# Four half units instead of three in each expert job beside the first layer

## The chip, the core and the metric

The kernel runs as one program on one core of a Trainium2 chip. The metric is the device time of one execution in microseconds (us), from the host's launch to the result in memory; lower is better. The core has five engines that run their own instruction streams in order and wait for one another through semaphores: PE (matmul; PEld is its weight load), ACT (ScalarE: activation functions), DVE (VectorE), POOL (GpSimd) and SP (SyncE, which issues nearly all DMAs here, in order).

## What is computed

The reference is a network of two layers on x of shape (4, 32, 96, 256), that is 4 batches of 3072 tokens with 256 channels. Cut to what matters:

```python
# layer 0: group norm, a selective-scan block along the 96 steps, then one along the 32 variables
x = x + conv(gn(x))
# layer 1: additive attention in each batch (3072 queries x 3072 keys, 32 hidden units)
t = tokens(x)
h = tanh(q[:, :, None, :] + k[:, None, :, :] + bh)
t = t + softmax(h @ Wa + ba) @ ln(t)
# then a mixture of 4 experts on ln(t), gated by graph attention over 1048576 edges
for e in range(4):
    hh = gelu(xn @ W1[e] + b1[e])            # 256 -> 512
    out = out + gate[e] * (hh @ W2[e] + b2[e])   # 512 -> 256
t = t + out
```

An expert's output without its gate depends on attention's result alone. Gates need the whole graph, and so all four batches.

## The kernel before

All arithmetic of the parts told of here is in float32. One program order is written out by hand for PE, ACT, DVE and POOL: generators hand out small steps, and the order in which they are called is the order on each engine.

**Stages.** Layer 0 works in 64 blocks of 384 tokens: for each batch eight blocks "t" (along the 96 steps) and eight blocks "d" (along the 32 variables); the first "t" block of the next batch stands before a batch's "d" blocks. Batch 0 runs alone. From then on attention of batch b runs beside layer 0 of batch b+1. `Attention.units` goes through 768 units a batch ("an entry"), each of them one tanh of 128x3072 on ACT (line 905) into one of three `th` buffers; the scores that read it (matmuls of line 878) are issued two units later. Each block of layer 0 has 48 slots, and a slot of layer 0 is issued beside one attention unit, half a slot at a time. When layer 0 is done, attention's fourth entry runs on with the sorting of edges on DVE (`Edges.sort`) and with `Experts.early`. Then the tail.

**Three places where experts are computed.** The 12288 tokens are 24 blocks of 512 tokens, and a unit is one block with one expert, 24 x 4 = 96 units in all.

- `Beside` (lines 1563 to 1660) is called at the end of every slot of layer 0. It holds at most one job at a time: (batch, expert, j). A job covers three half units, that is three times 256 tokens. At slot 31 of a block `choose` takes the next job, if the next entry's keys are not yet being made, the present entry's column is at least 40, and the job's batch is older than the present entry; the job then runs through slots 0 to 31 of the next block. It has no memory of its own for weights: W1 and W2 of the expert lie in columns 0 to 2047 of the 3072 columns of `krep`, the keys' place of the next entry, the transposed tokens `xt` and the bias `b2` in that entry's `qsel`. The hidden values `h` (3 half units x 4 x 256 columns) lie in `uab`, which the front of the next layer-0 block uses again from slot 32 on. `PRODUCTS` names the slots in which the matmuls of half a hidden layer (8 instructions in the trace) are issued (line 1637), one slot later DVE adds b1 and moves them to `h` (line 1624); after the second of a half unit `fetch` (line 1613) loads the next 256 tokens into the one `xt`. At slot `GELU` one activation goes over the whole of `h` (line 1643). `OUTPUTS` names the slots for the second layer (line 1648), one slot later DVE adds b2 (line 1629) and SP stores 128 KB to `kept`.
- `Experts.early` takes units of the first three batches that no job has done, in pairs with one expert, in entry 3. Weights lie in the unused `krep`; an expert is loaded when it changes, and this counts 4.0 us in the step's own pacing. Each pair ends with a `yield None`; the step runs until attention is done and the pair then begun is finished.
- The tail runs what is left: `tail` (lines 1821 to 1921) has an order by steps t, three steps a unit: PE's hidden layer and ACT's GELU in the unit's own three, PE's output layer one step later. The first units of a block whose gates are not there in time are stored to `kept` (line 1795 moves them); later ones are gated at once (lines 1798 and 1808). Between units stand the edges: per step so many gathers on POOL (line 1425, and 1127), one-hot products (lines 1465 to 1479) and, after each quarter of the edges, the gates of a batch (`gates_of`). When a batch's gates are there, each kept block of it is loaded (2 MB `all`, 512 KB `y`), added up on DVE with 16 operations (line 1808) and stored; two buffers each.

**What sets the number of jobs.** 12 half units a batch and expert give 4 jobs; two batches and four experts 32 jobs. Entry 1 has room for 13 jobs and entry 2 for 12, so 25 are run: 75 half units, 37 whole units. `early` then runs 22 units (11 pairs, three experts), and 37 stay for the tail, of which 17 are kept and 20 gated at once; 19 blocks are kept.

**Expert places.** `expert_places(t)` gives columns 0 to 1023 of a `krep` to W1 and 1024 to 2047 to W2; 1024 columns are free, which `early` uses in part for b2 and `Beside` not at all.

Of the kernel before, what the change touches and what calls it, by code (L numbers as in the profile page):

```python
# [21 lines left out]
AF = mybir.ActivationFunctionType  # L22
# [4 lines left out]
P = 128  # L27
B, NV, S, C = 4, 32, 96, 256
TOK = NV * S
M = B * TOK  # L30
NT = TOK // P
KC = C // P
# [18 lines left out]
HEADS, NEXP, FF = 4, 4, 512  # L51
# [10 lines left out]
HALVES = 3.0, 9.0  # L62
# [4 lines left out]
TB = 512  # L67
NQ, FC, NBLK_X = TB // P, FF // P, M // TB
# [5 lines left out]
class Layer0:  # L74
# [8 lines left out]
    def __init__(self, ctx, tc, ident, a, x1):  # L83
        self.nc, self.tc = tc.nc, tc
        self.ident, self.a, self.x1 = ident, a, x1
        pool = lambda name, bufs, **k: ctx.enter_context(tc.tile_pool(name=name, bufs=bufs, **k))
        self.const, self.wk, self.st = pool("l0c", 1), pool("l0w", 1), pool("l0s", 2)
        self.ps, self.ps_u = pool("l0p", 1, space=PSUM), pool("l0u", 1, space=PSUM)
        self.dram = pool("l0d", 1, space=bass.MemoryType.DRAM)
        self.ps_x = pool("l0x", 1, space=PSUM)  # L90
        self.turn, self.beside, self.dctx = 0, None, ctx.enter_context(ExitStack())
        self.dA = self.decay_places(True)
        self.lctx = ExitStack()
        alone = lambda name, **k: self.lctx.enter_context(
            tc.tile_pool(name=name, bufs=1, side="right", **k))
        self.ld, ps_l = alone("ldw"), alone("ldp", space=PSUM)
        self.dA.append(ps_l.tile([P, 1024], F32, tag="dA2", name="dA2"))
        self.lead_psum = lambda: ps_l.tile([P, 512], F32, tag="py", name="py")[:, :T]
        self.xt = [self.dram.tile([KC, P, NV, S], F32, tag="xt", name="xt", bufs=3)
                   for _ in range(B)]  # L100
        self.group_norm()
# [275 lines left out]
    def back(self, blk, then):  # L377
# [39 lines left out]
        def inputs(e, j):  # L417

            def f():
                if shared(j):  # L420
                    return
                dB = z["dB", j] = st.tile([P, SB, T], F32, tag="dB", name="dB", bufs=1)
                nc.vector.tensor_tensor(dB, blk["bB"].pop(j),  # L423
                                        z["dtu"].unsqueeze(1).to_broadcast([P, SB, T]), ALU.mult)
                fetch("bB", j)
            return f

        def inputs_beside(e, j):

            def f():  # L430
                dB = z["dB", j] = self.ld.tile([P, SB, T], F32, tag="dBl", name="dB", bufs=2)
                nc.gpsimd.tensor_tensor(dB, blk["bB"].pop(j),
                                        z["dtus", e].unsqueeze(1).to_broadcast([P, SB, T]), ALU.mult)
                fetch("bB", j)
            return f
# [16 lines left out]
        def outputs(j):  # L452
            def f():
                h = z["h", j]
                nc.gpsimd.tensor_tensor(h, h, blk["bC"].pop(j), ALU.mult)  # L455
                fetch("bC", j)
            return f
# [1093 lines left out]
def expert_places(t):  # L1551

    n = KC * FF
    return (t[:, :n].rearrange("p (k f) -> p k f", k=KC),
            t[:, n:n + FC * C].rearrange("p (k c) -> p k c", k=FC))


def load_expert(nc, a, e, w1, w2):
    nc.sync.dma_start(w1, a["W1"][e].rearrange("(k p) f -> p k f", p=P))
    nc.sync.dma_start(w2, a["W2"][e].rearrange("(k p) f -> p k f", p=P))  # L1560


class Beside:
# [2 lines left out]

    PRODUCTS = {0: (0, 0), 3: (0, 1), 5: (1, 0), 8: (1, 1), 10: (2, 0), 12: (2, 1)}
    GELU = 14  # L1570
    OUTPUTS = {15: (0, 0), 17: (0, 1), 20: (1, 0), 23: (1, 1), 26: (2, 0), 29: (2, 1)}

    def __init__(self, ctx, tc, a, l0, att, xn2T, dram):
        self.nc = nc = tc.nc
        self.a, self.l0, self.att, self.xn2T, self.dram = a, l0, att, xn2T, dram
        pool = ctx.enter_context(tc.tile_pool(name="l0e", bufs=1))
        self.o = lambda: pool.tile([P, C], F32, tag="eo", name="eo")
        self.b1 = pool.tile([P, NEXP, FC], F32, tag="eb1", name="eb1")
        nc.sync.dma_start(self.b1, a["b1"])
        self.half = TB // 2  # L1580
        n = TOK // self.half // 3
        self.jobs = [(b, e, j) for b in range(B - 2) for e in range(NEXP) for j in range(n)]
        self.kept, self.done, self.job, self.there = {}, [], None, None

    def units(self):

        halves = {(2 * (b * TOK // TB) + 3 * j + k, e) for b, e, j in self.done for k in range(3)}
        return [(i, e) for i in range(NBLK_X) for e in range(NEXP)
                if (2 * i, e) in halves and (2 * i + 1, e) in halves]

    def choose(self, last):


        att = self.att
        self.job = None
        if (not self.jobs or last or att.asked > att.entry + 1 or att.col < 40
                or self.jobs[0][0] >= min(att.normed, att.entry)):
            return
        b, e, j = self.job = self.jobs.pop(0)
        place = att.krep[(att.entry + 1) % 2]  # L1600
        self.w1, self.w2 = expert_places(place)
        rest = att.qsel[(att.entry + 1) % 2]
        self.xt, self.b2 = rest[:, :KC * self.half].rearrange("p (k m) -> p k m", k=KC), rest[:, KC * self.half:]
        if self.there != (att.entry, e):
            self.there = att.entry, e
            load_expert(self.nc, self.a, e, self.w1, self.w2)
            self.nc.sync.dma_start(self.b2, self.a["b2_rep"][:, e, :])
        self.first = 2 * (b * TOK // TB) + 3 * j
        self.fetch(0)

    def fetch(self, k):
        m = (self.first + k) * self.half
        self.nc.sync.dma_start(self.xt, self.xn2T[:, :, m:m + self.half].rearrange("k p m -> p k m"))

    def __call__(self, slot, last):
        nc = self.nc
        if self.job:
            b, e, j = self.job
            if slot == 0:
                self.h = self.l0.wide("eh").rearrange("p (k f m) -> p k f m", k=3, f=FC)  # L1620
            if slot - 1 in self.PRODUCTS:
                k, f2 = self.PRODUCTS[slot - 1]
                for f in (2 * f2, 2 * f2 + 1):
                    nc.vector.tensor_scalar(self.h[:, k, f, :], self.ps[:, f % 2, :],
                                            self.b1[:, e, f:f + 1], None, ALU.add)
            if slot - 1 in self.OUTPUTS:
                k, q = self.OUTPUTS[slot - 1]
                o = self.o()
                nc.vector.tensor_tensor(o, self.ps[:, 0, :], self.b2, ALU.add)
                i, n = divmod(self.first + k, 2)  # L1630
                nc.sync.dma_start(self.kept_block(i)[:, 2 * n + q, e, :], o)
            if slot in self.PRODUCTS:
                k, f2 = self.PRODUCTS[slot]
                self.ps = self.bank()
                for f in (2 * f2, 2 * f2 + 1):
                    for c in range(KC):
                        nc.tensor.matmul(self.ps[:, f % 2, :], self.w1[:, c, f * P:(f + 1) * P],
                                         self.xt[:, c, :], start=(c == 0), stop=(c == KC - 1))
                if f2 and k < 2:
                    self.fetch(k + 1)  # L1640
            if slot == self.GELU:
                h = self.h.rearrange("p k f m -> p (k f m)")
                nc.scalar.activation(h, h, AF.Gelu)
            if slot in self.OUTPUTS:
                k, q = self.OUTPUTS[slot]
                self.ps = self.bank()
                for f in range(FC):
                    nc.tensor.matmul(self.ps[:, 0, :], self.h[:, k, f, q * P:(q + 1) * P],  # L1648
                                     self.w2[:, f, :], start=(f == 0), stop=(f == FC - 1))
            if slot == 31:  # L1650
                self.done.append(self.job)
        if slot == 31:
            self.choose(last)
# [10 lines left out]
class Experts:  # L1664
# [54 lines left out]
    def hidden(self, i, w1, f):  # L1719

        ph = self.bank(self.ps_h, [P, TB], "ph")
        for k in range(KC):
            self.nc.tensor.matmul(ph, w1[:, k, f * P:(f + 1) * P], self.xts[i][:, k, :],
                                  start=(k == 0), stop=(k == KC - 1))
            yield ph
# [464 lines left out]
```

## Time and profile before

| what | us |
|---|---|
| median of 3 runs | 15007.42 (15002.35 to 15027.46) |
| the profiled execution's own time | 15006.76 |
| its span in the profile | 15004.8 |
| ACT busy in the span | 12227.7 (81%) |
| PE busy | 11632.7 (78%) |
| DVE busy | 10437.2 (70%) |
| POOL busy | 9042.6 (60%) |
| tanh of attention (L905), 3072 of them | 8667.0 |
| first and last GELU of a job (L1643) | 5620.8 and 10987.8 |
| first GELU of a tail unit (L1805) | 13936.6 |
| first and last edge gather (L1425) | 13942.1 and 14789.7 |
| last addition of a kept block (L1808) | 14983.4 |

The table of groups has, for an expert job, the following (line, engine, operation, tiles, shape, count; busy us, mean ns; idle time just before them and what ended it):

```profile
L1648 PE MATMUL ex<-krep,eh 128*128 128x256 f32 x1200 | 333.5, 426 | 55.0 <-ACT eh L1643 54.4 <-DVE eo L1629 0.5
L1637 PE MATMUL ex<-qsel,krep 128*128 128x256 f32 x1200 | 313.1, 406 | 30.5 <-DMA qsel<-xn2T 26.6 <-DVE pT L977 2.2 <-DVE h L448 1.6
L1624 DVE TENSOR_SCALAR eh<-ex,eb 128x256 f32<-128x256 f32 x300 | 130.6, 477 | 23.3 <-PE ex L1637 23.3
L1629 DVE TENSOR_TENSOR eo<-ex,qsel 128x256 f32<-128x256 f32 x150 | 62.3, 416 | 4.7 <-PE ex L1648 4.3 <-DMA kept<-eo 0.4
L1643 ACT ACTIVATE eh<-eh 128x3072 f32<-128x3072 f32 x25 | 69.2, 2768 | 0.3
```

The counts tell how much is done: 25 GELUs are 25 jobs, 1200 matmul instructions are 16 for each of 75 half units. Blocks of layer 0 can be told apart in the trace by their 64 decays (L410): blocks 25 to 32 go from 3525.7 to 4972.9 us, blocks 41 to 48 from 6532.1 to 8081.4.

```profile
3525.70:4972.90 1447.20, 1103.43 (x9479) 413.66 (x9475) 1107.04 (x1497) 1429.09 (x1082) 1097.37 (x784) 0.89 0.50 152
6532.10:8081.40 1549.30, 1286.58 (x10232) 546.59 (x10232) 1156.44 (x1641) 1480.39 (x1105) 1093.82 (x785) 0.92 0.50 151
```

These are two lines of the table of busy time by stretch: the stretch, its length, then the busy time and number of instructions of PE, PEld, DVE, ACT and POOL, the granted TensorE clock, the DMA engines' share and GB/s. The first eight blocks have no jobs, the second eight have one each.

### The profile page before, as it was taken

How to read it: one execution, taken by the hardware profiler on the slowest of the kernel's cores; microseconds unless marked ns; L12 is line 12 of the kernel's file. 1: busy time of each engine (PE TensorE's matmuls, PEld its weight loads, DVE VectorE, ACT ScalarE, POOL GpSimd, SP SyncE). 2: the span in 40 equal slices, each digit the busy share in tenths (PEclk: the TensorE clock that was granted, in tenths of full speed). 3: DMA queues.
4: the chain of work that ended last, by engine and by line, in shares of the span. 5: the costliest groups of instructions: out<-in, count | busy, mean ns of one | idle time of the engine just before them, and what ended most of it. 6: DMA issues, size and time to landing. Idle time of an engine off the chain costs nothing.

```text
span 15004.8 us, 223310 instructions
## 1 busy us (share of the span) xinstructions
PE 11632.7 (78%) x86496; PEld 5146.9 (34%) x86496; DVE 10437.2 (70%) x14862; ACT 12227.7 (81%) x9485; POOL 9042.6 (60%) x6971
## 2 busy tenths in 40 slices
PE   5676656777777778888887787888877888888888
PEld 2333322222222323333333333333333344433544
DVE  7888887777777877777777877577767633311367
ACT  3454538999999889999999899999988899999121
POOL 5777777777777777767676677477640144100683
PEclk8988978888888888899999889899988999999999
DMA  6777764445454544555454444355531000000224
GB/s 207 227 230 233 239 203 142 150 151 153 150 152 153 161 152 147 152 149 153 150 154 156 149 150 152 105 153 151 152 115 44 15 16 10 24 23 23 59 54 136
DMA packets 1197826, 1986.83 MB, mean 132 GB/s; under 512 B 411984, under 2 KB 645072, under 8 KB 1194320
## 3 DMA queue, kind: packets, MB, share of 16 engines
q1 hardware_dynamic: 1169104, 1967.10, 42.8%
q0 software_dynamic: 27648, 5.36, 0.7%
q8 instruction: 680, 11.14, 0.3%
q14 instruction: 394, 3.23, 0.1%
HBM read 1864.71 MB, written 107.35 MB: 131 GB/s over the span
## 4 chain that ended last, share of the span: by engine, by line
ACT 17%; PE 16%; DVE 7%; POOL 5%; issue 4%; DMA 1%; SPq 0%; DVEq 0%; ACTq 0%; POOLq 0%
ACT th L905 12%; PE pe L878 8%; POOL gs L1425 3%; PE pv L984 3%; ACT dA L410 2%; DVE h L448 1%; ACT pr L968 1%; POOL gd L1127 1%; PE ptw L975 1%; PE po L1731 1%; PE pz L517 1%; PE pc L1322 1%; DVE y L1808 0%; PE ex L1648 0%; DVE dB L423 0%
## 5 line engine op out<-in xcount | busy, mean ns | idle before, releaser
L905 ACT ACTIVATE th<-krep,qsel 128x3072 f32<-128x3072 f32 x3072 | 8667.0, 2847 | 377.0 <-PE pe L878 359.0
L878 PE MATMUL pe<-th,wa_blk 128*32 128x384 f32 x49152 | 5050.1, 539 | 1587.7 <-ACT pr L968 1361.7
L455 POOL TENSOR_TENSOR h<-h,bC 128x768 f32<-128x768 f32 x2048 | 3759.8, 1837 | 2586.0 <-DVE h L448 2187.4
L448 DVE TENSOR_TENSOR_SCAN h<-dA,dB 128x384 f32<-128x384 f32 x3008 | 2707.8, 942 | 988.7 <-ACT dA L410 717.2
L878 PEld LDWEIGHTS pe<-th,wa_blk 128*32 128x32 f32 x49152 | 1459.3, 116 | 4154.1 <-issue 1974.4
L423 DVE TENSOR_TENSOR dB<-bB,dtu 128x768 f32<-128x768 f32 x1912 | 1811.9, 948 | 172.0 <-ACT dtu L498 137.2
L462 POOL TENSOR_TENSOR h<-h 128x768 f32<-128x768 f32 x752 | 1419.6, 1888 | 53.6
L410 ACT ACTIVATE dA<-dt,t_A 128x380 f32<-128x380 f32 x2048 | 1124.7, 570 | 386.2 <-DVE h L448 296.5
L474 PE MATMUL py<-h,ident 128*128 128x384 f32 x2176 | 944.7, 567 | 490.8 <-POOL h L455 490.7
L410 ACT ACTIVATE dA<-dt,d_A 128x372 f32<-128x372 f32 x2048 | 1102.3, 562 | 146.4 <-DVE h L443 107.9
L984 PE MATMUL pv<-xn,pT 128*32 128x257 f32 x18432 | 1101.0, 387 | 129.5 <-DVE pT L977 128.7
L1043 POOL TENSOR_SCALAR sf<-sel,f 128x32 f32<-128x32 f32 x384 | 144.7, 398 | 1583.9 <-ACT f L1039 1481.5
L443 DVE TENSOR_TENSOR_SCAN h<-dA,dB 128x768 f32<-128x768 f32 x544 | 948.3, 1751 | 153.2 <-ACT dA L410 87.7
L977 DVE COPY pT<-ptw 128x512 f32<-128x512 f32 (+1 forms) x768 | 419.3, 546 | 738.3 <-PE ptw L975 737.8
L984 PEld LDWEIGHTS pv<-xn,pT 128*32 128x32 f32 x18432 | 580.2, 111 | 704.9 <-DVE pT L977 256.1
L464 POOL TENSOR_TENSOR y<-y,h 128x384 f32<-128x384 f32 x752 | 783.2, 1042 | 59.0
L463 POOL TENSOR_TENSOR h<-h 128x384 f32<-128x384 f32 x752 | 780.7, 1038 | 58.9
L474 PEld LDWEIGHTS py<-h,ident 128*128 128x128 f32 x2176 | 427.1, 212 | 970.1 <-POOL h L455 740.3
L961 DVE TENSOR_REDUCE nb<-pe 128x1 f32<-128x768 f32 x384 | 362.4, 944 | 405.7 <-PE pe L878 405.6
L1425 POOL DMA_INDIRECT gs<-tab_s,si x432 | 517.5, 1198 | 108.4 <-issue 108.4
L986 DVE COPY pvs<-pv 128x257 f32<-128x257 f32 x384 | 160.7, 419 | 603.4 <-PE pv L984 601.9
L1127 POOL DMA_INDIRECT gd<-tab_a,di x432 | 448.8, 1039 | 185.1 <-issue 182.0
(291 smaller groups left out, 15267.6 us busy)
## 6 DMA issues: line engine op xcount, KB each, us to landing
bB<-bc SPq DMA_DIRECT2D x2048, 384.0 KB
bC<-bc SPq DMA_DIRECT2D x2048, 384.0 KB
all<-kept SPq DMA_DIRECT2D x19, 2048.0 KB
x<-x SPq DMA_DIRECT2D x144, 256.0 KB
x<-x SPq DMA_DIRECT2D x192, 128.0 KB
xt<-xn2T SPq DMA_DIRECT2D x41, 512.0 KB
kept<-ko SPq DMA_DIRECT2D x39, 512.0 KB
qsel<-xn2T SPq DMA_DIRECT2D x75, 256.0 KB
```

The source lines that it names most:

```text
L410: nc.scalar.activation(inner(dA[:, s * T:(s + 1) * T] if alone else self.dA[s][:, :T]), inner(blk["dt"][:, e, :]), AF.Exp, scale=blk["w"][ ...
L423: nc.vector.tensor_tensor(dB, blk["bB"].pop(j), z["dtu"].unsqueeze(1).to_broadcast([P, SB, T]), ALU.mult)
L443: nc.vector.tensor_tensor_scan(flat(h), dA[:, :SB * T], flat(dB), 0.0, ALU.mult, ALU.add)
L448: nc.vector.tensor_tensor_scan(h[:, s, :], self.dA[s][:, :T], dB[:, s, :], 0.0, ALU.mult, ALU.add)
L455: nc.gpsimd.tensor_tensor(h, h, blk["bC"].pop(j), ALU.mult)
L462: nc.gpsimd.tensor_tensor(h0, h0, h1, ALU.add)
L464: nc.gpsimd.tensor_tensor(y[e], y[e], h0[:, 0, :], ALU.add)
L474: nc.tensor.matmul(z["py"], self.ident, h[:, s, :], start=(i == 0), stop=(i == DS - 1))
L878: nc.tensor.matmul(pe[q * QU:(q + 1) * QU, j, :KQ // 2], self.wa[:, k, :], th[:, c0:c0 + KQ // 2], start=(k == 0), stop=(k == NK - 1))
L905: nc.scalar.activation(th, s["krep"], AF.Tanh, bias=s["qsel"][:, col:col + 1])
L984: nc.tensor.matmul(pv[q * QU:(q + 1) * QU, :C + 1], pT[:, i, q * QU:(q + 1) * QU], s["xn"][:, q * NK + i, :], start=(i == 0), stop=(i == N ...
L1425: nc.gpsimd.indirect_dma_start(out=self.got[j][:, u, :], out_offset=None, in_=self.tab_s.rearrange("p n f -> (p n) f"), in_offset=bass.Ind ...
```

## The change

A job covers four half units. 12 half units a batch and expert give three jobs, so there are 24 jobs in all, twelve for each of the two batches. The hidden values of the fourth half unit do not lie in `uab` but in the last 1024 columns of the same `krep` that holds the expert's weights (`spare`, reached through `hidden(k, f)`). The GELU is two activations, one over the three half units in `uab` and one over `spare`, in slot 15 instead of 14. Products are issued in slots 0, 2, 4, 6, 8, 10, 11 and 13 (before: 0, 3, 5, 8, 10, 12), outputs in every second slot from 16 to 30 (before: 15, 17, 20, 23, 26, 29). The loads of `xt` follow the products of slots 2, 6 and 10. If all 24 jobs run, they cover 48 units; `early` chooses among 24 units, and with its 22 there are 26 for the tail.

```diff
-    PRODUCTS = {0: (0, 0), 3: (0, 1), 5: (1, 0), 8: (1, 1), 10: (2, 0), 12: (2, 1)}
-    GELU = 14
-    OUTPUTS = {15: (0, 0), 17: (0, 1), 20: (1, 0), 23: (1, 1), 26: (2, 0), 29: (2, 1)}
+    HALVES = 4
+    PRODUCTS = dict(zip((0, 2, 4, 6, 8, 10, 11, 13), ((k, f) for k in range(4) for f in range(2))))
+    GELU = 15
+    OUTPUTS = dict(zip(range(16, 32, 2), ((k, q) for k in range(4) for q in range(2))))
...
-        n = TOK // self.half // 3
+        n = TOK // self.half // self.HALVES
...
+        self.spare = place[:, KC * FF + FC * C:].rearrange("p (f m) -> p f m", f=FC)
...
-        self.first = 2 * (b * TOK // TB) + 3 * j
+        self.first = 2 * (b * TOK // TB) + self.HALVES * j
...
+    def hidden(self, k, f):
+        return self.h[:, k, f, :] if k < 3 else self.spare[:, f, :]
...
-                    nc.vector.tensor_scalar(self.h[:, k, f, :], self.ps[:, f % 2, :],
+                    nc.vector.tensor_scalar(self.hidden(k, f), self.ps[:, f % 2, :],
                                             self.b1[:, e, f:f + 1], None, ALU.add)
...
-                if f2 and k < 2:
+                if f2 and k + 1 < self.HALVES:
                     self.fetch(k + 1)
             if slot == self.GELU:
-                h = self.h.rearrange("p k f m -> p (k f m)")
-                nc.scalar.activation(h, h, AF.Gelu)
+                for h in (self.h.rearrange("p k f m -> p (k f m)"),
+                          self.spare.rearrange("p f m -> p (f m)")):
+                    nc.scalar.activation(h, h, AF.Gelu)
...
-                    nc.tensor.matmul(self.ps[:, 0, :], self.h[:, k, f, q * P:(q + 1) * P],
+                    nc.tensor.matmul(self.ps[:, 0, :], self.hidden(k, f)[:, q * P:(q + 1) * P],
                                      self.w2[:, f, :], start=(f == 0), stop=(f == FC - 1))
```

`units()` counts the finished half units with the same `HALVES`.

More of the change, by code (lines that the diff above doesn't have):

```diff
@@ L1585, in units @@
     def units(self):
-        halves = {(2 * (b * TOK // TB) + 3 * j + k, e) for b, e, j in self.done for k in range(3)}
+        halves = {(2 * (b * TOK // TB) + self.HALVES * j + k, e)
+                  for b, e, j in self.done for k in range(self.HALVES)}
         return [(i, e) for i in range(NBLK_X) for e in range(NEXP)
```

## The prediction

> **What bounds the kernel now.** I read the busy times by stage first, then the same table for the first 33 slots of four blocks, then what ScalarE waits for, then the chain of waits at the end. Columns of the tables: stretch, length, busy time (and instructions) of PE, PEld, DVE, ACT, POOL, then clock, DMA share, GB/s.
>
> ```profile
> 2200.00:5566.00 3366.00, 2448.32 (x20734) 958.90 (x20734) 2649.19 (x3655) 3159.88 (x2419) 2496.10 (x1781) 0.87 0.49 151
> 5566.00:11163.00 5597.00, 4507.69 (x36800) 1937.06 (x36804) 4153.44 (x5944) 5306.20 (x3913) 3828.89 (x2754) 0.90 0.49 148
> 11163.00:13936.60 2773.60, 2331.30 (x22861) 1048.86 (x22854) 1189.08 (x2096) 2520.78 (x1042) 442.79 (x757) 0.93 0.09 24
> 14733.50:15004.80 271.30, 223.90 (x676) 137.46 (x674) 196.52 (x407) 47.09 (x62) 48.67 (x43) 0.92 0.47 157
> ```
>
> Rows 1 and 2 are layer 0 beside attention, without and with expert jobs: ACT is busy 94 and 95%. Row 3 is attention alone with the early units. Row 4 is the tail from the first GELU of its 27th unit (14733.5). ACT rules until 13936, and there PE is next: 81% in row 2.
>
> ```profile
> 2620.20:2740.40 120.20, 91.32 (x826) 35.98 (x822) 92.61 (x120) 119.27 (x91) 93.25 (x68) 0.90 0.48 152
> 3707.90:3827.10 119.20, 98.89 (x830) 36.77 (x826) 88.65 (x120) 118.73 (x91) 92.38 (x66) 0.91 0.50 157
> 5566.10:5694.80 128.70, 109.20 (x890) 50.96 (x894) 96.83 (x138) 124.71 (x94) 92.27 (x67) 0.91 0.50 156
> 6726.50:6857.30 130.80, 117.45 (x902) 52.68 (x902) 94.77 (x137) 125.03 (x94) 92.26 (x67) 0.93 0.51 155
> ```
>
> Slots 0 to 32 of a "t" and a "d" block without a job, then with one. The job adds 8.5 and 11.6 us; PE's idle time falls from 28.9 to 19.5 ("t") and from 20.3 to 13.4 ("d"). ACT's idle time before tanh from 5566 to 11163 (what ended it, us, times):
>
> ```profile
>   PE pe L878: 163.9, 167
> ```
>
> The same row of 2240 to 5566, without jobs, says 25.4 us in 52 places. The first stretch has 1394 tanhs, the second 834; at the second's rate the first would wait 25.4 x 1394/834 = 42.5 us; the other 121.4 us, over 25 jobs (75 fetches of xt, 3 each), are **4.9 us a job** in which ScalarE waits for the matmuls that a job put ahead of attention's.
>
> **Stage B, one job fewer.** Blocks 41 to 48 ("d", jobs) last 1549.3/8 = 193.7 us, blocks 25 to 32 (none) 1447.2/8 = 180.9. Entry 1 now ends its 12 jobs at block 47, so block 48 has none: **-12** (bounds -11 and -13).
>
> **Stage B, the fourth half unit, 24 times.** ACT: GELU takes 2764 ns for 3072 columns (L1643) and 1909 for 2048 (L1767), so 855 per 1024 and some 0.2 for a second instruction: **1.05** a job (0.9 to 1.1). No further table load: both GELUs follow one another.
>
> ```profile
> 5619.46 1.28 ACT L1643 ACT_TABLE_LOAD   x1
> 5620.76 2.77 ACT L1643 ACTIVATE eh<-eh 128x3072 f32<-128x3072 f32 x1
> 5623.43 2.84 ACT L905 ACTIVATE th<-krep,qsel 128x3072 f32<-128x3072 f32 x1
> 5626.29 1.28 ACT L410 ACT_TABLE_LOAD   x1
> ```
>
> A job's fixed ACT cost is thus two loads, 2.6 us, with nothing idle around them; this is in the -12. The Trainium skill ("ScalarE: Activation LUTs", "What ACT_TABLE_LOAD costs") puts about 1.38 us of drain beside each 1.28 us load; the rows above show none, and by the rule the job saved would be worth 2.8 us more.
>
> PE: 16 matmuls more for products (313.1/75 = 4.2 us a half) and 16 for outputs (333.5/75 = 4.4): 8.6 us more in 33 slots that have 13 to 19 idle, part of it waiting for GELU (PE waits for L1643 54.4 us in 21 places) and not to be had. Proportionally ACT would wait 4.9/3 = 1.6 more a job; at worst all 8.6; at best nothing, if it all fits into the idle time. Waits grow faster than the load: I take **2.5**, nearer to the proportional row. The extra DVE work (4 x 0.48 + 2 x 0.42 = 2.8 us) lies in VectorE's 28% idle share; if that cover were gone it would cost up to 2.8 a job.
>
> The fetch of the fourth xt: issued after the products of slot 10 and used in slot 11, where earlier fetches had two slots. A fetch of today, two slots ahead:
>
> ```profile
> 5787.31 2.00 PE L1637 MATMUL ex<-qsel,krep 128*128 128x256 f32 x8
> 5789.85 2.85 ACT L905 ACTIVATE th<-krep,qsel 128x3072 f32<-128x3072 f32 x1
> 5790.55 0.42 SPq L1613 DMA_DIRECT2D qsel<-xn2T  x1
> 5793.60 2.85 ACT L905 ACTIVATE th<-krep,qsel 128x3072 f32<-128x3072 f32 x1
> 5795.02 1.75 PE L1637 MATMUL ex<-qsel,krep 128*128 128x256 f32 x7 [1.50 <-DMA qsel<-xn2T]
> ```
>
> The matmuls end at 5789.3, SyncE issues 1.2 us later (bC and xt stand ahead of it in its queue) and the data is there 4.5 us after that: 7.7 us from product to product, where one slot offers 3.75. PE stalls 2.8 to 4.0 us, about 3.4. Behind it in PE's queue stand the next scores (L878), for whose end tanh waits, with three th buffers of slack; in SP's queue the fetch holds up the bB and bC loads behind it until the products end, as each fetch does today (VectorE waits 4.6 us in all for bB in this stretch). Today's waits of 1 to 2 us hardly show in ACT; I take **1.0** of the 3.4 (bounds 0 and 3.4). The Trainium skill ("DMA: Bandwidth & Descriptors", "Anatomy of one DMA") fits about 2.0 us fixed plus bytes/436e3 per us, here 2.6 us, for copies issued by GpSimd; the row of this SyncE fetch says 4.5 under load and decides. By the rule the stall would be some 1.5 and I would take 12 us less.
>
> The two stores of eo more a job (8 for 6) go down SP's queue between bB and bC loads; DMA waits before L1629 are 0.4 us in all, so nothing, or up to 0.4 us x 24 if each costs as much as all do now. Expert loads stay 8 pairs (4 an entry). The spare place is part of the same krep tile as the weights: if the order is kept for whole tiles, products of slot 13 wait for the additions of slot 12 (0.9 us) and outputs of slot 16 for the second GELU (0.9); a slot lies between, so nothing, at most 1.8 a job. Sum B: -12 + 24 x (1.05 + 2.5 + 1.0) = **+97** (at best 24 x 0.9 - 13 = +9, at worst 24 x 13.1 - 11 = +303, the whole of PE's work on the path).
>
> **Stage C.** The early step has 24 units to choose from instead of 35 and runs 11 pairs as before, but in four experts instead of three: one load more, with 4.0 us in its own pacing; after the last tanh so much more of the pair is left to do: **+4** (0 to 10).
>
> **The tail.** Units 1 to 26 run in the same steps, so nothing falls away before 14733. Thereafter:
>
> ```profile
> 14769.25 4.09 DMA gs<-tab_s,si
> 14786.79 3.46 PE po L1731 x16
> 14806.24 3.43 PE ph L1723 x8
> 14864.43 11.53 DMA out<-y
> 14875.98 3.33 DMA y<-x
> ```
>
> The chain is the edge gather until 14769, then the last quarter's sums with unit matmuls pushed between (14786 to 14824: 3.46 + 3.43 + 1.72 + 3.46 = 12 us, their VectorE operations 3), then the last gates (until 14860; 6 us of unit operations among them). From there it is store, load of the next y, 16 additions (7.9 us) with two buffers: (11.5 + 3.3 + 1 + 7.9)/2 = 12 us a kept block. Nine and a half blocks remain at 14860, 114 us, today 124 between units' work. So of 11 units (15 us of PE each, 165) only 12 + 3 + 6 + 10 come off, and the last units' overhang of kept blocks (14984 to 14999), 15: 46. Against it 22 instead of 19 kept blocks: three more in the gather's stretch, 3 x 7.9 = 24 us of VectorE, of which I count 4 (0 to 15). **-42** (-25 to -60).
>
> Sum: 97 + 4 - 42 = **+59**; 15006.8 (the profiled execution, 0.6 below the median of the runs) + 59 = **15066**.
>
> **Rivals.** (1) Only proportional waits, 1.6 and 0.3 a job: B = -12 + 24 x 2.95 = 59, tail -50: 15006.8 + 59 + 4 - 50 = 15020. For it: today's DMA waits of PE are 26.6 us in 23 places. (2) PE becomes the bound of job blocks: in 15 "d" blocks 8.6 + 3.4 = 12 of 13.4 us idle would have to be usable. If ACT waits 8 of the 12 there and 5 in 9 "t" blocks, B = -12 + 24 x 1.05 + 165 = 178 and the time 15006.8 + 178 + 4 - 42 = 15147. Against it: PE's idle in "t" is 19.5. (3) **Faster**: PE's idle time swallows the half unit and the fetch (0 wait), at blocks 36 to 47 and 52 to 63: B +9, tail -60, C 0: 14956. It decides where a job adds under 2.1 us in all (12 + 42 - 4 over 24), that is under 1.0 of waiting. Against it: the 4.9 of today. (4) It doesn't do what it says: a job is not taken in time, or early ends a pair sooner (28 units): some +10 on the forecast; opportunities were 13 and 12 for 12 and 12 jobs, so hardly.
>
> **Numbers.** Forecast 0.42 (own range 15037 to 15110), (1) 0.22, (2) 0.20, (3) 0.13, (4) 0.03. Range: 14985 to 15150 leaves out most of (3) and half of (2). About 0.2%, 30 us, is what a measurement here tells from no change: faster 0.13, same 0.24 ((1) and a little of the forecast's lower end), slower 0.63.
>
> **What would show it.** Job blocks of 195 to 199 us ("d") where they were 193; ACT's wait for L878 in the second stretch up from 164 to some 240 us; a PE wait for xt of 3 us in slot 11, 24 times; in the tail the last gates some 25 us sooner, counted from its first GELU, and kept blocks still 12 us apart. Wrong if job blocks stay within 2 us of today's, or if kept blocks close up.

## The result, and the profile after

The changed kernel takes **15223.51 us** (median of 4 runs, 15202.15 to 15237.15), the kernel before 15004.89 us (4 runs, 14998.33 to 15027.46): ratio 1.0142, 95% interval 1.0124 to 1.0159, slower by 1.4%. The prediction said slower, with 15066 us: about a quarter of the loss that came, and its range ended at 15150. The profiled execution after took 15229.7 us, its span is 15227.8.

By stage, each time read from the two traces (us from the span's start):

| | before | after | difference | predicted |
|---|---|---|---|---|
| first tanh of entry 3 (end of layer 0) | 11464.9 | 11707.4 | +242.5 | +97 |
| from there to the last tanh (stage C) | 2406.0 | 2405.4 | -0.6 | 0 |
| last tanh to first tail GELU | 65.7 | 69.7 | +4.0 | +4 |
| first tail GELU to the end | 1068.2 | 1045.4 | -22.8 | -42 |

11 of the 242 us are there already at block 36, before the first job (5566.1 and 5577.1); the rest, +231, arises between the first job and the end of layer 0. (In the traces of all twelve kernels block 36 begins between 5560.2 and 5577.1, so the 11 are scatter.) Units for the tail fell from 37 to 26 and kept blocks rose from 19 to 22, as the change says; 24 jobs ran.

The rows that answer to those of the prediction are first ScalarE's idle time before tanh in the stretch with jobs (5577 to 11400): what ended it, us, times.

```profile
  PE pe L878: 382.9, 221
```

Before, this row said 163.9 in 167 places: **219 us more**, nearly the whole of the +231. ScalarE's busy time is hardly the cause: in the table of groups tanh itself has 8674.8 us after and 8667.0 before. The other half of the story is what PE waited for ahead of the products of a job (line 1643, formerly 1637):

```profile
  DMA qsel<-xn2T: 101.9, 23
```

That was 26.6 us, also in 23 places; now each wait is 4.4 us, and it sits where the prediction put it, before the seventh product, in slot 11. Here is that slot in block 37, in the timeline (start, duration, engine, line, operation, then in brackets the idle time before it and its releaser; SPq is SyncE's issue):

```profile
5815.22 1.99 PE L1643 MATMUL ex<-qsel,krep 128*128 128x256 f32 x8
...
5818.82 0.32 SPq L373 DMA_DIRECT2D bC<-bc  x1
...
5819.23 0.38 SPq L373 DMA_DIRECT2D bB<-bc  x1
...
5819.70 0.39 SPq L1616 DMA_DIRECT2D qsel<-xn2T  x1
...
5824.53 3.75 PE L1643 MATMUL ex<-qsel,krep 128*128 128x256 f32 x8 [5.15 <-DMA qsel<-xn2T]
...
5832.61 2.86 ACT L905 ACTIVATE th<-krep,qsel 128x3072 f32<-128x3072 f32 x1 [6.96 <-PE pe L878]
```

The products that free `xt` end at 5817.2. SyncE issues its load only at 5819.7, because two other loads stand ahead of it in its queue; the data is there 4.8 us later. PE stands idle for 5.15 us, then needs 3.75 us for eight matmuls such as took 1.99 just before, and the scores behind them (line 878) release the next tanh 6.96 us late. The busy times of these moments (stretch, length, PE, PEld, DVE, ACT, POOL, clock, DMA share, GB/s) say why the matmuls became slow:

```profile
5815.20:5819.40 4.20, 3.88 (x30) 2.05 (x26) 3.79 (x5) 4.20 (x5) 2.12 (x2) 1.00 0.36 94
5819.40:5824.50 5.10, 0.00 (x0) 0.00 (x0) 2.23 (x5) 5.10 (x2) 3.73 (x3) 0.74 0.88 253
5824.50:5828.20 3.70, 3.67 (x8) 2.50 (x8) 0.00 (x0) 1.15 (x3) 2.88 (x3) 0.50 0.14 46
```

The granted clock is 1.00 before the idle time and **0.50** after it; in the next 4.4 us it is back at 0.94. Over the 24 jobs the seventh product takes 3.52 us on average, and in 23 of them it runs at the lower clock for most or all of its time (2.92 to 3.75 us). The Trainium skill ("TensorE: Matmul & The Clock Gate", "Part 1: The HAM clock gate (the "warmup" mystery)") says that the clock falls to a half after an idle window of about 3.4 us and comes back after as long a busy one. The rows above, with 5.1 us of idle time, agree. But shorter idle times did it too: five of the 24 stalls lasted 2.6 to 2.8 us, and after four of them the product took 2.92 to 3.75 us.

Blocks with a job grew from 193.3 to 203.8 us ("d") and from 190.9 to 201.0 ("t"), 10 us instead of the predicted 4.55 (without blocks 40, 55 and 63, which last longer in both kernels). Blocks 41 to 47, all "d" with a job, in the same columns (blocks 41 to 48 of before, all with a job, stand above at 193.7 us a block):

```profile
6589.30:8029.60 1440.30, 1189.24 (x9176) 533.41 (x9176) 1028.79 (x1473) 1304.31 (x974) 954.61 (x685) 0.90 0.47 145
```

1440.3/7 = 205.8 us a block, of which ACT is busy 186.3 and PE 169.9. ACT had 185.0 of 193.7 before (1480.39/8). So ScalarE's work grew by 1.3 us a block and its idle time by 10.8: ScalarE is still the fullest engine, but it now stands idle for 19.4 us of a block instead of 8.6. Split by slots, a "t" block gains 1.4 us in slots 0 to 8, **7.8 in slots 9 to 12** (around the fetch), 0.9 in slots 13 to 16 (the GELU) and nothing after; a "d" block 1.5, 4.1, 2.2 and 2.5.

In the tail, the stretch after the last gates:

```profile
15094.00:15227.80 133.80, 0.00 (x0) 0.00 (x0) 74.45 (x160) 0.00 (x0) 0.00 (x0) 0.50 0.66 219
```

160 VectorE operations are 10 kept blocks (16 each), 13.4 us a block, with VectorE busy for only 7.4 of them. No unit is left here, PE has nothing to do at all. Before, the same stretch was 144.7 us, with PE busy for 113.27. The timeline of VectorE and the chain of waits (start, duration, tile) show what sets the pace:

```profile
15124.87 15.75 DVE L1815 SCALAR_TENSOR_TENSOR y<-all,gates,y 128x256 f32<-128x256 f32 x32 [12.93 <-DMA y<-x]
15151.94 15.76 DVE L1815 SCALAR_TENSOR_TENSOR y<-all,gates,y 128x256 f32<-128x256 f32 x32 [11.31 <-DMA y<-x]
```

```profile
15133.19 9.58 DMA out<-y
15142.79 9.02 DMA y<-x
```

Blocks go in pairs, one pair every 27 us: add up two (15.8), then wait while one is stored (9.6) and the next y is loaded into its place (9.0, and 9.9 in the following pair).

### The profile page after: what moved, and what is told of

It reads as the page before. It is cut to its first block, busy times and chain, and to the rows that moved or that the text cites. A ratio compares the mean times of both kernels' runs of the same rounds, so it can differ in the third digit from the quotient of the medians.

```text
span 15227.8 us, 223806 instructions
## 1 busy us (share of the span) xinstructions
PE 11630.4 (76%) x86640; PEld 5183.9 (34%) x86640; DVE 10490.2 (69%) x14966; ACT 12223.4 (80%) x9453; POOL 9039.5 (59%) x6971
## 4 chain that ended last, share of the span: by engine, by line
PE 18%; ACT 16%; DVE 6%; POOL 5%; issue 4%; DMA 1%; SPq 0%; DVEq 0%; ACTq 0%; POOLq 0%
ACT th L905 11%; PE pe L878 8%; PE pv L984 3%; POOL gs L1425 2%; ACT dA L410 2%; DVE h L448 1%; PE ptw L975 1%; ACT pr L968 1%; PE ex L1643 1%; POOL gd L1127 1%; PE po L1738 1%; DVE y L1815 1%; PE ex L1655 1%; PE px L236 1%; PE pc L1322 0%
## 5 line engine op out<-in xcount | busy, mean ns | idle before, releaser
L905 ACT ACTIVATE th<-krep,qsel 128x3072 f32<-128x3072 f32 x3072 | 8674.8, 2851 | 597.7 <-PE pe L878 580.3
L975 PE MATMUL ptw<-ident,pr 128*128 128x128 f32 x2304 | 479.6, 326 | 111.3 <-DVE pT L977 42.5
```

The lines of the kernel that those rows point to most:

```text
L905: nc.scalar.activation(th, s["krep"], AF.Tanh, bias=s["qsel"][:, col:col + 1])
```

## The experiments

Two questions were open: which part of a job's longer time makes ScalarE wait, and why the whole of it comes through. The theories are named by letters in the expectations. **A**: the fetch of the fourth `xt`, one slot ahead of its use, stalls PE, and the stall passes whole to ScalarE. **B**: it is the mass of PE's work, 32 matmuls a job. **C**: it is two products in adjacent slots, whatever the fetch does. Later **S**: the stall reaches ScalarE because the order leaves the three `th` buffers no slack; **T** is its rival, under which that order makes no difference. All kernels were timed against the one before; medians are in us, with the ratio and its 95% interval.

**1. Two slots for the last fetch.** The seventh product stays at slot 11, the sixth goes from slot 10 to 9, so that every fetch has two slots.

```diff
-    PRODUCTS = dict(zip((0, 2, 4, 6, 8, 10, 11, 13), ((k, f) for k in range(4) for f in range(2))))
+    PRODUCTS = dict(zip((0, 2, 4, 6, 8, 9, 11, 13), ((k, f) for k in range(4) for f in range(2))))
```

> Theory A (the fetch that is used one slot after it is issued costs ScalarE some 6 us a job: a wait of PE of 5 us, matmuls at half rate after it): products in slots 0, 2, 4, 6, 8, 9, 11, 13 give every fetch two slots again, 24 x 6 = 144 us less than the changed kernel, about 15080 us (15055 to 15110). Theory B (it is the 32 matmuls more a job in PE's queue, wherever they stand): nothing to speak of, 15190 us or more.

Measured: 15133.94 (15121.86 to 15143.84), 1.0089 [1.0072, 1.0106]: 90 us less than the changed kernel, 3.7 a job (80 us by the two ratios). PE's waits for `xt` fell:

```profile
  DMA qsel<-xn2T: 27.6, 12
```

Slots 9 to 12 take 17.96 us in a "t" block and 16.86 in a "d" block, against 22.15 and 19.49 in the changed kernel and 14.32 and 15.41 before. The seventh product takes more than 2.5 us in 6 of 24 jobs instead of 23. A is right in kind and too large in size: it explains 90 us, not the 144 that it claimed.

**2. No load of the fourth `xt`.** The change as it is, but the fourth half unit is computed on the third's tokens.

```diff
-                if f2 and k + 1 < self.HALVES:
+                if f2 and k + 1 < 3:
```

> The changed kernel without the load of the fourth xt: the fourth half unit is computed from the third one's tokens, so the outputs of a quarter of the half units are those of others; all matmuls stay in their slots 10, 11 and 13. Theory A: the same saving as by moving the products, about 15075 us. Theory B: 15190 us or more. A third one (C), that two products in neighbouring slots wait for one PSUM bank: little here (above 15150 us), but all of it by moving the products.

Measured: 15129.90 (15125.59 to 15135.43), 1.0084 [1.0067, 1.0101], 94 us less than the changed kernel (87 by the two ratios) and the same as experiment 1. The products of slots 10 and 11 still stand side by side here, so C doesn't explain these 90 us: taken away or given a second slot, the fetch is worth the same. But the wait that C names is there: PE now waits 51.4 us for VectorE's additions, 50.0 of them in 24 places before the seventh product, until the one `ex` bank is free, and in 11 of the 24 jobs that product still takes more than 2.5 us. (In experiment 1 the products of slots 8 and 9 are such neighbours.) What this costs by itself no run separates. Against the changed kernel PE has lost 56 us less in idle time before the seventh products and 23 us less in slow matmuls, 79 in all; the stretch from block 36 to the end of layer 0 is 89 us shorter (6041.5 against 6130.3). So what the fetch cost PE came through whole.

**3. A late fetch in the kernel before.** The reverse: three half units, but one product a slot earlier, so that the last fetch (after slot 8) has one slot.

```diff
-    PRODUCTS = {0: (0, 0), 3: (0, 1), 5: (1, 0), 8: (1, 1), 10: (2, 0), 12: (2, 1)}
+    PRODUCTS = {0: (0, 0), 3: (0, 1), 5: (1, 0), 8: (1, 1), 9: (2, 0), 12: (2, 1)}
```

> The kernel before, three half units a job, with the first product of the third half unit in slot 9 instead of 10, so that its fetch has one slot instead of two. Theory A: 25 jobs x some 6 us more than before, about 15150 us (15100 to 15190). Theory B: as many matmuls as before, 15005 us (within 20).

Measured: 15086.73 (15080.82 to 15094.84), 1.0056 [1.0039, 1.0072]. One slot less costs the kernel before 88 us, 3.5 a job over 25 jobs, without a single instruction more. PE's waits for `xt`, 26.6 us in 23 places before:

```profile
  DMA qsel<-xn2T: 74.8, 24
```

B, which expected nothing, fails for this part; A's +150 is again too large. The idle time is 3.1 us a job, and 17 of 25 products take more than 2.5 us (2 of 25 before). The products of slots 8 and 9 are neighbours here, so a wait for the bank may be hidden behind the one for `xt`; this run doesn't tell the two apart.

**4. Neither the fetch nor the fourth half unit's matmuls.** Experiment 2, and the fourth half unit's 32 matmuls are left out too; GELU, additions and stores stay (VectorE reads other tiles in place of PSUM). The edit makes VectorE slower: the additions of line 1630 for the fourth half unit take 1299 ns on average instead of 476, and from block 36 to the end of layer 0 VectorE is busy for 4553 us, where experiment 2 has 4458.

```diff
-                    nc.vector.tensor_scalar(self.hidden(k, f), self.ps[:, f % 2, :],
+                    nc.vector.tensor_scalar(self.hidden(k, f), self.ps[:, f % 2, :] if k < 3 else self.h[:, 2, f, :],
...
-            if slot in self.PRODUCTS:
+            if slot in self.PRODUCTS and self.PRODUCTS[slot][0] < 3:
...
-            if slot in self.OUTPUTS:
+            if slot in self.OUTPUTS and self.OUTPUTS[slot][0] < 3:
```

> The changed kernel without the fourth fetch and without the 32 matmul instructions of the fourth half unit (VectorE makes its operations from other data, so GELU, additions and stores stay, and the fourth half units' outputs are other numbers). Theory A: below the kernel without the fourth fetch by what the matmuls cost, 24 x 2 to 3 = 50 to 70 us: about 15010 us. Theory B: the whole of stage B's excess but GELU's 25 us goes, 24 x 8 = 190 less than the changed kernel, about 15030 us, and the kernel without the fourth fetch stands at 15190 or more.

Measured: 15040.02 (15017.27 to 15053.52, 9 runs), 1.0025 [1.0014, 1.0035]: 90 us less than experiment 2, **3.7 a job** for the 32 matmuls and the wait for the bank, which goes with them; VectorE's longer work may hide a part of the gain. B is right for this part. The profiled execution is the fastest of the nine, 23 us below their median. In it the stretch from block 36 to the end of layer 0 is 5945.9 us, where before it is 5898.8; ScalarE's waits for line 878 in it are 246.5 against 223.9, so 23 of these 47 us; GELU's 24 x 1.05 less the 5.3 of one job saved explain another 20. What the 23 comes from, products and outputs standing closer, fewer quiet slots or the longer additions, no run separates.

**5. Scores one unit after tanh instead of two, in the changed kernel.** With `LAG` 2, the scores that free a `th` buffer are issued shortly before the tanh that needs it. With 1 they are issued one tanh earlier. The constant moves more than that: the softmax of an attention unit and the loads of values that follow the scores also come one slot earlier beside the slots of layer 0 and of the jobs.

```diff
-LAG = 2
+LAG = 1
```

> The changed kernel with the scores one attention unit behind their tanh instead of two, so that a th buffer comes free one slot sooner in PE's order. Theory S (a stall of PE passes whole into ScalarE because three th buffers with a lag of two leave it no slot to run ahead): the late fetch's 3.7 us a job are mostly absorbed, 60 to 150 us less than the changed kernel, about 15110 us. Theory T (PE has no idle time to catch up in, so its stalls pass on whatever the slack): within 40 us of 15220.

Measured: 15056.20 (15055.84 to 15066.83), 1.0047 [1.0031, 1.0062]: **167 us less** than the changed kernel (143 by the two ratios), of which by the trace 111 in the stages up to entry 3 (100 of them after block 36) and 54 in stage C. PE's waits for `xt` are what they were, 101.5 us, but over the span ScalarE waits only 67.2 us for line 878, where it was 580.3; now PE is the one that waits for tanh (867.2 us, where it was 225.0). That doesn't make the stall free. ScalarE's waits from block 36 to the end of layer 0 (us, times, longest), first in the changed kernel:

```profile
ACT th L905 <- PE pe L878: 439.6, 251, 9.2
ACT dA L410 <- DVE h L448: 64.2, 99, 5.0
```

and with the scores one unit behind:

```profile
ACT dA L410 <- DVE h L448: 244.0, 193, 6.0
ACT pr L968 <- DVE nb L961: 144.1, 54, 11.9
ACT th L905 <- PE pe L878: 50.5, 26, 5.8
```

The row of line 968 was 38.1 us. So 389 us of waits for PE are gone, and 286 us of waits for VectorE have come. How much of the fetch's price the slack absorbs is told by experiment 10, which has the same lag and two slots for every fetch (its third change acts in the tail): it needs 5976.8 us for this stretch, experiment 5 needs 6030.0, so the late fetch still costs **53 us**. With the old lag it cost 86 (6130.3 against 6044.7 in experiment 1). Only about a third is absorbed; the larger part of what the lag brings, 68 us, comes with the fetch in two slots too (6044.7 to 5976.8). T falls, since the time does change. S holds for the waits of tanh, but its "mostly absorbed" fails: the larger part of the stall reaches ScalarE by way of VectorE, whose two rows above are together 58 us smaller in experiment 10 (198.6 and 131.4).

**6. The same in the kernel before.** The edit is that of experiment 5.

> The same on the kernel before, so that what the lag alone does is known. Theory S: ScalarE's 359 us of waits for the scores become some 100 to 200 less, 14850 to 14950 us. Theory T: within 40 us of 15000; more than that above if PE now waits for tanh instead.

Measured: 14948.32 (14938.09 to 14966.58, 7 runs), 0.9969 [0.9958, 0.998]. ScalarE's wait for line 878 goes from 359.0 to 61.4 us, yet the gain is 48 us, the least that S allowed and little more than T did: 43 of it in stage C, none beside layer 0 (the first tanh of entry 3 comes 10 us later, not sooner, in an execution 18 us slower than the median). There the waits only changed their name. With the third `y` buffer added (experiment 9) the stretch from block 36 to the end of layer 0 still takes 5894.3 us, and ScalarE's largest waits in it are for VectorE, 165.9 where they were 70.2 and 104.0 where they were 45.6, while those for line 878 fell from 223.9 to 43.4:

```profile
ACT dA L410 <- DVE h L448: 165.9, 190, 5.5
ACT pr L968 <- DVE nb L961: 104.0, 49, 11.7
```

**7. A third place for y in the tail**, on top of experiment 1.

```diff
-        y = self.io.tile([P, NQ, C], F32, tag=tag, name="y")
+        y = self.io.tile([P, NQ, C], F32, tag=tag, name="y", bufs=3 if tag == "y2" else 2)
```

> The kernel with two slots for every fetch, and three y buffers instead of two for the kept blocks of the tail. If after the last gates the kept blocks wait for store, then load of y, in two buffers (13.5 us a block), the last stretch of 128 us falls to some 105 to 115 and the time by 10 to 25 us against the same kernel with two (15134). If the 2 MB loads bound it (3 MB at 219 GB/s is 13.7 us), it stays within 5 us.

Measured: 15091.42 (15082.93 to 15105.47), 1.0066 [1.0051, 1.0081], 43 us less than experiment 1, more than was expected. In the traces the stretch after the last gates falls from 129.0 to 100.1 us, so 29 of the 43 are the buffer's; the rest lies within the scatter of single runs. VectorE's timeline, to be held against the pairs shown of the changed kernel:

```profile
15050.84 7.92 DVE L1815 SCALAR_TENSOR_TENSOR y<-all,gates,y 128x256 f32<-128x256 f32 x16 [2.04 <-DMA y<-x]
15061.11 7.92 DVE L1815 SCALAR_TENSOR_TENSOR y<-all,gates,y 128x256 f32<-128x256 f32 x16 [2.35 <-DMA y<-x]
```

A block now every 10 us, with waits of some 2. Store, load and additions one after the other in two buffers set the pace of the tail's end.

**8. More room for the fetches of the kernel before.** Three half units, each fetch three slots ahead of its use.

```diff
-    PRODUCTS = {0: (0, 0), 3: (0, 1), 5: (1, 0), 8: (1, 1), 10: (2, 0), 12: (2, 1)}
+    PRODUCTS = {0: (0, 0), 2: (0, 1), 5: (1, 0), 7: (1, 1), 10: (2, 0), 12: (2, 1)}
```

> The kernel before with products in slots 0, 2, 5, 7, 10, 12 instead of 0, 3, 5, 8, 10, 12: both fetches have three slots. If today's fetches of two slots still cost ScalarE something (PE waits 26.6 us in 23 places for xt), 10 to 30 us less than before, some 14980 us; if two slots are enough, no difference within 10 us.

Measured: 15014.50 (15003.91 to 15032.39, 11 runs), 1.0013 [1.0004, 1.0022]. The expectation fails: PE's waits for `xt` all but vanish (1.8 us in 3 places) but nothing is gained (if anything it is a little slower), and ScalarE's wait for line 878 is 370.2 us over the span, not less than the 359.0 of before. So taking away the short waits that two slots leave (1.2 us each) brought nothing that could be measured, where one slot cost 3.5 us a job. The edit isn't free of side effects, though: with two products a slot earlier, slots 0 to 8 take 1.4 us more in a "t" block and 0.8 in a "d" block, which may cover a gain.

**9. Three half units with both repairs**: the kernel before, `LAG` 1, three places for y.

> The kernel before (three half units a job) with the scores one unit behind their tanh and with three y buffers for kept blocks. If both gains stand beside each other: 48 us and some 10 to 20 less than before, about 14930 us; the tail's end is partly set by units' matmuls in this kernel, so the y buffer brings less than the 29 us it brought beside four half units.

Measured: **14916.61** (14914.49 to 14938.41, 5 runs), 0.9947 [0.9933, 0.9961]: 80 us less than the kernel before, a little more than the 58 to 68 expected. It beats both kernels.

**10. Four half units with both repairs**: experiment 1 with `LAG` 1 and three places for y.

> Four half units a job with two slots for every fetch, the scores one unit behind, three y buffers: the changed kernel under the best conditions found. If the lag already absorbs the late fetch, moving it brings 10 to 30 us and the y buffer 29: 15056 less 50, about 15005 us (14985 to 15025), still above three half units under the same conditions by 60 us or more. If the two are independent, 15056 - 90 - 29 = 14940 us, level with them.

Measured: 14965.59 (14957.16 to 14982.42, 11 runs), 0.9979 [0.997, 0.9988], between the two expectations: of the 91 us below experiment 5 the y buffer has some 29, and the moved fetch some 60. With the slack and the tail mended, and the fetch too but for 42.8 us in which PE still waits for `xt`, four half units lose 49 us to three. By the traces the tail gains 29.5 (1008.3 us against 1037.8), and the stretch from block 36 to the end of layer 0 loses 82.5 (5976.8 against 5894.3). ScalarE's waits in that stretch, against those shown at experiment 6:

```profile
ACT dA L410 <- DVE h L448: 198.6, 190, 6.8
ACT pr L968 <- DVE nb L961: 131.4, 50, 11.6
```

33 and 27 us more, 10 more for line 878 (53.0 against 43.4), and GELU's 20: about that loss (other waits fell by 4). Waiting for PE has turned into waiting for VectorE. Whether VectorE is late by its own 2.8 us more a job or because PE feeds it later wasn't separated. A fourth `th` buffer wasn't tried.

## Why the prediction was right in sign and wrong in size

**Job by job.** "One job fewer -12": block 48 went from 191.2 to 183.3 us, so -8. "GELU 1.05": slots 13 to 16 of a "t" block grew by 0.9, and the second activation takes 1042 ns. Stage C's +4 came as 4.0. These two hold; the first is 4 us short, beyond its bounds of -11 and -13.

**The step that failed: "Today's waits of 1 to 2 us hardly show in ACT; I take 1.0 of the 3.4."** The stall itself was placed right, to the slot, with its 23 or 24 occurrences; its size was 4.4 us instead of 3.4 (the load waits longer behind bC and bB in SP's queue). What failed is the share that passes on. Experiments 1 and 2 measure it: 80 to 94 us, 3.3 to 3.9 us a job, which is all that PE lost there (79 us in experiment 2); experiment 3 finds 88 us in the kernel before. Two things were missing. The stall has a tail of its own: the eight matmuls after it run at clock 0.50 and take 1.5 us longer. And the text counted "three th buffers of slack", but with scores issued two units late all three buffers are in use. That this is the reason why the whole of it came through is shown only in part: with one unit less of lag ScalarE's waits for the scores are nearly gone, but 53 of the fetch's 86 us are still paid, now as waits for VectorE. That second path the prediction didn't have; behind the stall shown above VectorE stood idle for 9.69 us until PE's products of line 984 were there. Small waits were taken as a scale for large ones; experiment 8 took the small ones away and gained nothing, so they gave no scale that could be relied on.

**"Waits grow faster than the load: I take 2.5."** The right mechanism and a term too small: experiment 4 gives 3.7 a job for the 32 matmuls, of the at most 8.6. In it is the wait for the bank between the products of slots 10 and 11 (2.1 us of idle PE a job in experiment 2), on which the prediction put no price; how the 3.7 divide between the two is open. About 1 us a job more (23 us in all) remains when fetch and matmuls are both gone; the prediction put no price on products and outputs every second slot either.

**The sum of stage B.** In ratios to the kernel before, the fetch's removal takes 1.0142 to 1.0084 and the matmuls' 1.0084 to 1.0025: 0.58 and 0.59% of 15000, 87 and 89 us, or 3.6 and 3.7 a job, where the forecast had 1.0 and 2.5. The two differences, 24 x (2.6 + 1.2) = 91, are most of the 134 by which +97 fell short of +231; the rest are the 23 that experiment 4 leaves open, the 4 of block 48 and some 15 us that no run assigns.

**The tail, -42.** -23 came. The gather ended at the same time after the first GELU (854.0 and 853.1), as assumed; the last gates came 911.5 instead of 923.5 us after it, 12 sooner and not 21; the last stretch is 11 shorter, not 25. The step "12 us a kept block" counted the load of y at 3.3 us; the same chain of the kernel before also has loads of y of 9.02, 4.21 and 9.97 us, so the shortest of four was taken. In the stretch after the last gates such a load takes 7.8 to 11.0 us and a block 13.4. Experiment 7 confirms the place.

**The rivals.** (2), PE as bound, came nearest in time (15147) and named the same places, but not the mechanism: it had PE's idle time used up, and in the "d" blocks shown above PE stands idle for 35.9 us a block, where it was 32.8; with another order of the same work (experiment 5) 100 us of the loss beside the jobs go away. (3), the faster one, set 1.0 us of waiting a job as its border; even with the late fetch gone, the matmuls and the wait for the bank cost 3.7. (1) assumed proportion; the waits for `xt` went from 1.2 to 4.4 us each, but what they cost went from nothing that experiment 8 could measure to 3.3 to 3.9 us a job. (4) is out: jobs, units and blocks are as the change says.

## What to carry to other kernels

Before a stall on one in-order engine is costed at a fraction, count how far the engines that it feeds can run on without it: buffers less the units that the order itself keeps in flight. Here that was next to nothing, and the stall counted whole. Count it for every engine that is fed: one slot more of slack for ScalarE took away its waits for PE, but more than half of the stall's price stayed, by way of VectorE. And a wait that vanishes from the profile isn't yet time won: in the kernel before, 298 us of waits went and 48 us were gained. Spreading fetches that already fit gained nothing; pulling the next use a single slot too close cost 3.5 us a job.

## What the runs showed of the hardware

- A PE that stood idle for 5.15 us ran the next eight matmuls at clock 0.50, 3.75 us instead of 1.99, in the middle of a stretch with mean clock 0.90. After 23 of the 24 stalls of 2.6 to 6.6 us the eight took 2.92 us or more. Without the fetch (experiment 2), where 23 of 24 idle times before them are 1.4 to 2.4 us, they took more than 2.5 us in 11 jobs of 24.
- A 256 KB load issued by SyncE was usable 4.8 us after its issue, and had stood 2.5 us behind two others whose turn came first. A 512 KB load of y took 7.8 to 11.0 us beside other transfers at the end of the changed kernel, and 3.3 to 10.0 us in the tail of the kernel before.
- VectorE's additions of 128x256 values for the fourth half unit took 458 to 484 ns reading PSUM (experiment 2) and 346 to 2008 ns, 1299 on average, reading other tiles at the same places (experiment 4).
